# One state of each scan step in layer 3 multiplied with C by TensorE and ScalarE, and two small matmuls split over row groups

## The chip, the cores and the metric

The kernel runs on one core of a Trainium2 chip. The core has TensorE (PE, matmuls into PSUM), VectorE (DVE), ScalarE (ACT), GpSimd (POOL) and SyncE (SP, which here issues the DMA transfers). The engines run side by side, each through its own list of instructions in order, and wait for each other by semaphores. The metric is the device time of one execution in microseconds (us).

## The reference

Four layers are applied one after the other to an image of 8 x 64 x 64 x 64 float32. The change lies in layer 3, which holds two passes of a bidirectional selective scan: over one image axis, then over the other. For each direction, cut to what matters:

```
xn = rms_norm(x);  xz = xn @ ipw.T;  xc, z = split(xz)          # 64 -> 2 x 256 channels
xc = silu(causal_dwconv(xc))                                     # 4 taps along the sequence
dbl = xc @ xpw.T                                                 # 4 (dt) + 16 (B) + 16 (C) values per token
dt = softplus(dbl[:4] @ dtw.T + dtb)                             # 256 channels
h_t[d, n] = exp(dt_t[d] * A[d, n]) * h_{t-1}[d, n] + dt_t[d] * xc_t[d] * B_t[n]     # n = 0..15
y_t[d] = sum over n of h_t[d, n] * C_t[n]
y = (y + D * xc) * silu(z);  y @ opw.T
```

A sequence has 64 tokens. There are 256 inner channels d and 16 states n. C_t[n] depends on the token and the state only, not on the channel.

## The kernel before, in words

**Tiling.** Layer 3 works in *steps*: `steps` holds 2 passes (s) x 16 chunks (c) x 4 groups (g) x 2 directions (k) = 256 of them. A step takes 512 tokens (eight sequences) and all 256 channels of one direction. A tile is [128, 1024]: 128 channels on the partitions, and along the row 512 tokens of channels 0 to 127 (j = 0), then the same 512 tokens of channels 128 to 255 (j = 1). For each of the 16 states one such tile is worked through.

**The loop.** `stream` (line 433) is shared by layers 1, 2 and 3. Its iteration `i` is one state of one step, `i = 16 * step + n`; it writes out the order of all instructions by hand. Per state the work is:

- `fetch` (SP): the row of B and C of this state is loaded from HBM, broadcast to 128 partitions, six states ahead (tile `bc`, eight buffers).
- `multiply_b` (POOL, line 484): `hb = du * B`, three states ahead, four buffers.
- `decay` (ACT, line 491): `dA = exp(dt * A[n])`, two activations of 512, into one of two PSUM buffers, issued for state i + 2 at the end of iteration i.
- `scan` (DVE, line 500): the recurrence, over `dA` and `hb`. For most states its result overwrites `dA`. For a *shared* state it goes to an SBUF tile `h` (three buffers), so that the PSUM buffer is free as soon as the scan ends.
- `multiply_c` (line 514): the product with C. DVE does it for most states (into `hc`, four buffers) right after the scan; POOL does it for the states listed in `Step.shared`, in the next iteration, after that iteration's `multiply_b`.
- `gather` (PE, line 306): the product is added to the PSUM tile `acc` by two 128x512 matmuls with the identity, two iterations later. At state 0 of the next step it first drains the finished sum: `drain` (DVE, line 2074) multiplies `acc` with silu(z). At state 2 this stands behind the scan, and `acc` has one buffer.

In layer 3 the shared states are (1, 4, 7, 10, 13), and (2, 6, 10, 14) where k = 1 and g is odd.

**What else goes through the loop.** `prepare` (line 1999) computes the next step's inputs in pieces, one piece in an iteration, from state 1 on: tap matmuls (2009), silu to `u` (2021), the B, C, dt projection (2024), its copy `dbl` and its store to HBM (2027, 2030), the dt matmuls (2033, four rows of weights), softplus (415), `du` (POOL, 2044), the z matmuls (2047, 64 rows of weights), silu to `z` (2057). A piece of ACT work that needs another table of functions is marked `CALM` and is held back until `calm(i)` says that neither state i nor i + 1 is shared. Other pieces come from two queues that `advance` (line 417) steps once per iteration: `urgent`, in which `finish` (line 2087) stands once a k = 1 step is done (output matmuls 2093 and 2096, then an activation that writes the output tile, 2112), and `behind`, in which `begin` (line 1925) loads and normalises the next chunk. All these pieces share one PSUM tile `mm` (pool `pp`, one buffer of two banks): a piece that yields True holds it, and no other may take it until it is released.

Of the kernel before, what the change touches and what calls it, by code (L numbers as in the profile page):

```python
# [10 lines left out]
F32 = mybir.dt.float32  # L11
AF = mybir.ActivationFunctionType
ALU = mybir.AluOpType
# [5 lines left out]
C = 64  # L19
HW = 64  # L20
L = HW * HW
NS = 16
T = 1024
# [83 lines left out]
def layouts(i):  # L107
    o = {"x": i["x"].reshape(NP, 128, L)}
# [19 lines left out]
    p = "L1_conv_"  # L128
# [26 lines left out]
    p = "L2_conv_"  # L155
# [6 lines left out]
    xp = i[p + "ssm_xproj_w"]  # L162
# [12 lines left out]
    p = "L3_conv_"  # L175
# [8 lines left out]
    o["l3_xp"] = i[p + "x_proj_w"].reshape(4, 36, 2, 128).transpose(3, 0, 2, 1)  # L184
    o["l3_dtw"] = i[p + "dt_proj_w"].reshape(4, 256, 4).transpose(2, 0, 1)
# [83 lines left out]
class Net:  # L269
# [163 lines left out]
    def stream(self, pools, ahead, steps, behind, rest=None):  # L433
# [18 lines left out]
        nc = self.nc  # L452
        bp, hbp, hcp, hp, pe, pa = pools
        total = len(steps) * NS
        B, CC, hb, dA, hc, acc = {}, {}, {}, {}, {}, {}

        def need(i, what):

# [34 lines left out]
        def shared(i):  # L493
            return i % NS in steps[i // NS].shared

        def scan(i):
            s, n = steps[i // NS], i % NS
            h = hp.tile([128, T], F32, name="h") if shared(i) else dA[i]
            way = slice(None, None, -1) if s.rev else slice(None)
            nc.vector.tensor_tensor_scan(h[:, way], dA[i][:, way], hb.pop(i)[:, way], s.first(n), ALU.mult, ALU.add)  # L500
            dA[i] = h
            if shared(i):
                s.keep(n, h)

        def calm(i):

# [10 lines left out]

        def gather(i):
            at, n = divmod(i, NS)
            if n == 0:  # L520
                if at:
                    steps[at - 1].drain(acc.pop(at - 1))
                    steps[at - 1].done()
                acc[at] = pa.tile([128, T], F32, name="acc")
                begun[at] = steps[at].skip(acc[at])
            self.mm(acc[at], self.ident, hc.pop(i), start=n == 0 and not begun[at], stop=n == NS - 1)
# [12 lines left out]
        for i in range(total + 2):  # L539
            at, n = divmod(i, NS)  # L540
            need(i + ahead[0], "bc")
            need(i + ahead[1], "du")
            fetch_c(i + ahead[2])
            fetch(i + ahead[0])
            multiply_b(i + ahead[1])
            if 0 < i <= total and shared(i - 1):
                multiply_c(i - 1)


            first = i > NS and n == 2  # L550
# [12 lines left out]
            room = work is None or work.said is not True and (n < steps[0].early or hasattr(steps[at + 1], "du"))  # L563
            self.advance(behind, room, calm(i))
            if late:
                gather(i - 2)
            if i < total:
                scan(i)
            if first:
                gather(i - 2)  # L570
            if i < total:
                if not shared(i):
                    multiply_c(i)
            decay(i + 2)
        steps[-1].drain(acc.pop(len(steps) - 1))
# [288 lines left out]
    def layer1(self, src, dst):  # L864
        nc, tc, d = self.nc, self.tc, self.d
        mid = self.hbm["x1a"]
        with ExitStack() as ctx:
# [339 lines left out]

            class Step:
                start, early, late = 2, 8, True
                shared = (1, 4, 7, 10, 13)  # L1210
                shaped = staticmethod(lambda t: t)

                def __init__(self, b, k, j):
# [313 lines left out]
    def l2_scan(self, hx, hy):  # L1527
        nc, tc, d = self.nc, self.tc, self.d
        with ExitStack() as ctx:
# [35 lines left out]

            class Step:
                bc_shape, start, early, late = [128, 2, T], 2, 0, False
                shared = (1, 4, 7, 10, 13)
                rev = False
                behind = None  # L1570
                shaped = staticmethod(lambda t: t)
# [247 lines left out]
    def layer3(self, src, dst):  # L1819
# [8 lines left out]
        with ExitStack() as ctx:  # L1828
# [12 lines left out]
            class Weights:  # L1841
# [12 lines left out]
                def load(self):  # L1854
# [19 lines left out]
                    both = cp.tile([128, 2, 256], F32, name=f"both{s}")  # L1874
                    self.dtw, self.z = self.take("dtw", both[:4]), both[C:]
                    self.dtb, self.A, self.D = self.take("dtb"), self.take("A"), self.take("D")

                def build(self):
# [22 lines left out]
                                ALU.mult,  # L1901
                            )
                    for k in range(2):
                        nc.vector.tensor_scalar(
                            self.z[:, k, :], self.w_in[C:, k, 256:], self.nw[C:, k : k + 1], None, ALU.mult
                        )
# [74 lines left out]
            class Step:  # L1981
# [6 lines left out]
                def __init__(self, s, c, g, k):  # L1988
                    self.s, self.c, self.g, self.k, self.rev = s, c, g, k, k == 1
                    self.w = weights[s]  # L1990
                    self.shared = (2, 6, 10, 14) if k and g % 2 else (1, 4, 7, 10, 13)
                    self.lanes = [(slice(j * W, j * W + W), self.w.A[:, k, j, :]) for j in range(2)]

                def ready(self):
# [4 lines left out]
                def prepare(self):  # L1999
# [19 lines left out]
                    for j in range(2):  # L2019
                        at = slice(j * W, j * W + W)  # L2020
                        nc.scalar.activation(u[:, at], px[:, at], AF.Silu, bias=w.cb[:, k, j : j + 1])  # L2021
                    pd = pp.tile([128, T], F32, name="mm")[:36, :W]
                    for j in range(2):
                        nc.tensor.matmul(pd, w.xp[:, k, j, :], u[:, j * W : j * W + W], start=j == 0, stop=j == 1)  # L2024
                    yield True
                    dbl = p2.tile([36, W], F32, name="dbl")
                    nc.scalar.copy(dbl, pd)
                    self.bc = hp.tile([NS, 2, W], F32, name="bc")
                    for m in range(2):
                        nc.sync.dma_start(self.bc[:, m, :], dbl[4 + m * NS : 4 + m * NS + NS])  # L2030
                    pt = pp.tile([128, T], F32, name="mm")
                    for j in range(2):
                        nc.tensor.matmul(
                            pt[:, j * W : j * W + W], w.dtw[:, k, j * 128 : j * 128 + 128], dbl[0:4], start=True, stop=True
                        )
                    yield True
                    yield CALM
# [117 lines left out]
```

## Time and profile before

| | us |
|---|---|
| median of 3 runs | 24,518.06 (24,506.06 to 24,526.78) |
| the profiled execution | 24,525.61 |
| its span, first to last instruction | 24,523.8 |
| layer 3 within it | about 11,290 to 24,510 |

Busy shares of the whole span, from the page: PE 85%, DVE 91%, ACT 60%, POOL 90%. How to read it: engine rows give the line of the kernel, the operation, the tile written and the tiles read, the shapes and the count, then busy time and mean duration, then the idle time just before these instructions and what ended it. A float32 matmul appears as two `MATMUL` records (two passes), each with its weight load on the row of PEld. Matmul records are pipelined and overlap, so that the distance from start to start is what a pass costs. A timeline row gives the start, the duration, and in brackets how long the engine stood idle before it.

### The profile page before, as it was taken

The numbers are of one execution on the slowest core, as the hardware profiler recorded it, in microseconds if no ns is written. First come the engines' busy times: TensorE is split into PE (matmuls) and PEld (weight loads), VectorE is DVE, ScalarE is ACT, GpSimd is POOL, SyncE is SP. The second block draws the span as 40 slices with busy tenths as digits, with TensorE's granted clock in tenths as the row PEclk, the third lists the DMA queues.
The fourth block names the chain that finished last, engine by engine and source line by source line (L and its number), as shares of the span: only waits on it lengthen the run. The fifth ranks groups of instructions, "written<-read, shape, count | busy, mean of one in ns | idle before, by whom it ended". The sixth has DMA issues, their size and how long they took to land. (4 is left out here: it accounts for less than half of the span.)

```text
span 24523.8 us, 192937 instructions
## 1 busy us (share of the span) xinstructions
PE 20916.6 (85%) x53146; PEld 8080.3 (33%) x53146; DVE 22352.9 (91%) x12956; ACT 14733.5 (60%) x18824; POOL 22093.4 (90%) x10580
## 2 busy tenths in 40 slices
PE   7778888888888888898888888888888888888888
PEld 5323333333333223222333333333333333333333
DVE  5599999999999689978999999999999999999999
ACT  5445555555555456525666666666666666666666
POOL 0499999999999579967999999999999999999999
PEclk9889999999999999999999999999999999999999
DMA  2699889889888589923555555555555554555454
GB/s 76 198 328 319 314 314 322 313 314 318 315 311 310 173 284 338 321 54 120 173 168 171 171 172 168 172 170 170 171 169 172 170 172 169 172 169 173 168 174 157
DMA packets 1835292, 5282.68 MB, mean 215 GB/s; under 512 B 533712, under 2 KB 539924, under 8 KB 1831904
## 3 DMA queue, kind: packets, MB, share of 16 engines
q1 hardware_dynamic: 1809632, 5207.00, 62.8%
q10 hardware_dynamic: 24576, 63.33, 0.7%
q8 instruction: 423, 6.93, 0.1%
q14 instruction: 661, 5.41, 0.1%
HBM read 5112.85 MB, written 156.11 MB: 215 GB/s over the span
## 5 line engine op out<-in xcount | busy, mean ns | idle before, releaser
L484 POOL TENSOR_TENSOR hb<-du,bc 128x1024 f32<-128x1024 f32 x4608 | 10775.2, 2376 | 215.9 <-DVE h L500 143.7
L306 PE MATMUL acc<-hc,ident 128*128 128x512 f32 x18560 | 8782.1, 614 | 91.8 <-DVE img L1271 53.7
L491 ACT ACTIVATE dA<-dt,w_A 128x512 f32<-128x512 f32 x8192 | 5658.5, 691 | 3947.5 <-DVE hc L514 2892.5
L500 DVE TENSOR_TENSOR_SCAN dA<-dA,hb 128x1024 f32<-128x1024 f32 x3320 | 7579.2, 2283 | 199.0 <-ACT dA L491 114.9
L306 PE MATMUL acc<-h,ident 128*128 128x512 f32 x8064 | 4663.0, 707 | 2408.4 <-POOL h L514 2375.8
L306 PEld LDWEIGHTS acc<-hc,ident 128*128 128x128 f32 x18560 | 3638.5, 200 | 5214.5 <-issue 4560.6
L484 POOL TENSOR_TENSOR hb<-du,b 128x1024 f32<-128x1024 f32 x2048 | 4834.2, 2390 | 490.5 <-DVE dA L500 215.9
L514 DVE TENSOR_TENSOR hc<-dA,bc 128x1024 f32<-128x1024 f32 x3232 | 3954.9, 1224 | 244.7 <-issue 4.9
L491 ACT ACTIVATE dA<-dt,w_l_A 128x1024 f32<-128x1024 f32 x2560 | 2856.8, 1117 | 1001.4 <-DVE hc L514 761.1
L500 DVE TENSOR_TENSOR_SCAN h<-dA,hb 128x1024 f32<-128x1024 f32 x1416 | 3227.9, 2280 | 79.9 <-ACT dA L491 79.0
L514 POOL TENSOR_TENSOR h<-h,bc 128x1024 f32<-128x1024 f32 x1376 | 3264.8, 2373 | 8.0 <-DVE h L500 8.0
L306 PEld LDWEIGHTS acc<-h,ident 128*128 128x128 f32 x8064 | 1572.6, 213 | 5133.1 <-POOL h L514 3445.9
L500 DVE TENSOR_TENSOR_SCAN dA<-dA,carry,hb 128x1024 f32<-128x1024 f32 x1320 | 3093.1, 2343 | 116.5 <-POOL hb L484 45.1
L514 DVE TENSOR_TENSOR hc<-dA,c 128x1024 f32<-128x1024 f32 x1408 | 1722.9, 1224 | 116.8 <-DMA c<-bc 6.9
L514 POOL TENSOR_TENSOR h<-h,c 128x1024 f32<-128x1024 f32 x640 | 1518.5, 2373 | 8.2 <-ACT carry L1254 7.4
L491 ACT ACT_TABLE_LOAD x1128 | 1447.2, 1283 | 20.0
L500 DVE TENSOR_TENSOR_SCAN h<-dA,carry,hb 128x1024 f32<-128x1024 f32 x600 | 1404.2, 2340 | 36.6 <-ACT dA L491 25.5
L1254 ACT COPY carry<-dA 128x1 f32<-128x1 f32 x1056 | 167.6, 159 | 1646.7 <-DVE hc L514 1606.5
L2009 PE MATMUL mm<-xn,taps 128*128 128x512 f32 x2048 | 933.9, 598 | 1.1 <-ACT z L2057 1.1
L2044 POOL TENSOR_TENSOR du<-dt,u 128x1024 f32<-128x1024 f32 x256 | 607.6, 2374 | 9.8 <-ACT dt L415 9.8
L2024 PE MATMUL mm<-u,w_xp 128*36 128x512 f32 x1024 | 489.3, 600 | 139.1 <-ACT u L2021 132.3
L726 POOL MEMSET xf<- 128x24 f32 x33 | 4.3, 142 | 657.4 <-PE ps L747 494.4
(320 smaller groups left out, 17864.0 us busy)
## 6 DMA issues: line engine op xcount, KB each, us to landing
bc<-bc SPq DMA_DIRECT2D x4096, 512.0 KB
b<-bc SPq DMA_DIRECT2D x2048, 512.0 KB
c<-bc SPq DMA_DIRECT2D x2048, 512.0 KB
bc<-bc SPq DMA_DIRECT2D x512, 1024.0 KB
tmp<-rs SPq DMA_DIRECT2D x93, 512.0 KB
raw<-x SPq DMA_DIRECT2D x64, 512.0 KB
inv<-rs SPq DMA_DIRECT2D x64, 512.0 KB
tmp<-x SPq DMA_DIRECT2D x192, 128.0 KB
```

The lines of the kernel that those rows point to most:

```text
L306: self.nc.tensor.matmul(o, lhsT, r, start=start, stop=stop)
L484: nc.gpsimd.tensor_tensor(s.shaped(hb[i]), s.shaped(s.du), B.pop(i), ALU.mult)
L491: nc.scalar.activation(dA[i][:, cut], s.dt[:, cut], AF.Exp, scale=A[:, n : n + 1])
L500: nc.vector.tensor_tensor_scan(h[:, way], dA[i][:, way], hb.pop(i)[:, way], s.first(n), ALU.mult, ALU.add)
L514: engine.tensor_tensor(s.shaped(o), s.shaped(h), CC.pop(i), ALU.mult)
L726: nc.gpsimd.memset(x[:, :, HW:], 0.0)
L1254: nc.scalar.copy(self.carry[:, n : n + 1], h[:, last : last + 1])
L2009: nc.tensor.matmul(tokens(px[:, j * W : j * W + W]), w.taps[k][:, m, j * 128 : j * 128 + 128], xn[:, :, f : f + HW], start=m == 0, stop=m ...
L2024: nc.tensor.matmul(pd, w.xp[:, k, j, :], u[:, j * W : j * W + W], start=j == 0, stop=j == 1)
L2044: nc.gpsimd.tensor_tensor(du, dt, u, ALU.mult)
```

## The change

- Each step of layer 3 gets a list `turned = (13,)`. A turned state is scanned into an `h` tile like a shared one, but is multiplied with C in another way, by the generator `turn`: eight matmuls take 128x128 blocks of `h` as weights against the identity, so that the tile stands transposed in `mm`, tokens on the partitions; four activations on ACT copy it to SBUF, each scaled per partition by C of that token (`ct`); eight more matmuls with the copied blocks as weights turn it back and add it to `acc`.
- `turn` is put at the head of `urgent` when the state has been scanned. Its first piece takes the tile `mm` and yields `CALM`. Before the last state of the step is gathered, `gather` steps the queues until `turn` is over.
- The shared states become (1, 4, 7, 10), and (0, 3, 6, 9, 11) where k = 1 and g is odd. `calm` is unchanged.
- `ct` is loaded once per step from the stored C, 512 values of four bytes, as [128, 4].
- The dt matmuls use partitions 0 to 3 for the first 128 channels and 64 to 67 for the second (so the projection writes the four dt values twice, 68 rows); the z matmuls use partitions 0 to 63 and 64 to 127. The weights of both lie in one tile `both`.

Layers 1 and 2 have an empty `turned` list. In the changed kernel the lines are shifted: 2112 becomes 2153, 2074 becomes 2115, 306 becomes 307, 500 becomes 504.

```
@@ stream
+        def turned(i):
+            return i % NS in steps[i // NS].turned
+
         def scan(i):
             s, n = steps[i // NS], i % NS
-            h = hp.tile([128, T], F32, name="h") if shared(i) else dA[i]
+            h = hp.tile([128, T], F32, name="h") if shared(i) or turned(i) else dA[i]
...
+            if turned(i):
+                del CC[i]
+                turns[i] = Task(turn(i, dA.pop(i)))
+                self.urgent.appendleft(turns[i])
+
+        def turn(i, h):
+            s = steps[i // NS]
+            ps = s.pp.tile([128, T], F32, name="mm")
+            for m in range(4):
+                for j in range(2):
+                    at, o = j * 512 + m * 128, (m * 2 + j) * 128
+                    nc.tensor.matmul(ps[:, o : o + 128], h[:, at : at + 128], self.ident, start=True, stop=True)
+            yield CALM
+            o = hcp.tile([128, T], F32, name="hc")
+            for m in range(4):
+                at = slice(m * 256, m * 256 + 256)
+                nc.scalar.activation(o[:, at], ps[:, at], AF.Copy, scale=s.ct[:, m : m + 1])
+            yield False
+            for m in range(4):
+                for j in range(2):
+                    at, f = j * 512 + m * 128, (m * 2 + j) * 128
+                    nc.tensor.matmul(acc[i // NS][:, at : at + 128], o[:, f : f + 128], self.ident, start=False, stop=False)
...
         def gather(i):
             at, n = divmod(i, NS)
+            if turned(i):
+                return
+            if n == NS - 1:
+                for m in steps[at].turned:
+                    while not turns[at * NS + m].over:
+                        self.advance(behind)
...
-                if not shared(i):
+                if not shared(i) and not turned(i):
                     multiply_c(i)
@@ layer 3, Step
-                    self.shared = (2, 6, 10, 14) if k and g % 2 else (1, 4, 7, 10, 13)
+                    self.turned, self.pp = (13,), pp
+                    self.shared = (0, 3, 6, 9, 11) if k and g % 2 else (1, 4, 7, 10)
...
-                    pd = pp.tile([128, T], F32, name="mm")[:36, :W]
+                    pd = pp.tile([128, T], F32, name="mm")[:68, :W]
...
                     for j in range(2):
+                        at = slice(j * C, j * C + 4)
                         nc.tensor.matmul(
-                            pt[:, j * W : j * W + W], w.dtw[:, k, j * 128 : j * 128 + 128], dbl[0:4], start=True, stop=True
+                            pt[:, j * W : j * W + W], w.both[at, k, 128 - j * 128 : 256 - j * 128], dbl[at], start=True, stop=True
                         )
...
+                    self.ct = p2.tile([128, 4], F32, name="ct")
+                    for n in self.turned:
+                        nc.sync.dma_start(self.ct, self.bc[n, 1].rearrange("(m p) -> p m", p=128))
...
-                            w.z[:, k, j * 128 : j * 128 + 128],
-                            xn[C:, :, 4 : 4 + HW],
+                            w.both[j * C : j * C + C, k, j * 128 : j * 128 + 128],
+                            xn[j * C : j * C + C, :, 3 + j : 3 + j + HW],
```

More of the change, by code (lines that the diff above doesn't have):

```diff
@@ L183, in layouts @@
     o["l3_cb"] = i[p + "conv_b"].reshape(4, 2, 128).transpose(2, 0, 1)
-    o["l3_xp"] = i[p + "x_proj_w"].reshape(4, 36, 2, 128).transpose(3, 0, 2, 1)
-    o["l3_dtw"] = i[p + "dt_proj_w"].reshape(4, 256, 4).transpose(2, 0, 1)
+    xp = i[p + "x_proj_w"].reshape(4, 36, 2, 128).transpose(3, 0, 2, 1)
+    o["l3_xp"] = np.concatenate([fill(xp, (128, 4, 2, 64)), xp[..., :4]], axis=3)
+    o["l3_dtw"] = i[p + "dt_proj_w"].reshape(4, 2, 128, 4).transpose(3, 1, 0, 2)
     o["l3_dtb"] = i[p + "dt_proj_b"].reshape(4, 2, 128).transpose(2, 0, 1)
@@ L454, in stream @@
         total = len(steps) * NS
-        B, CC, hb, dA, hc, acc = {}, {}, {}, {}, {}, {}
+        B, CC, hb, dA, hc, acc, turns = {}, {}, {}, {}, {}, {}, {}
         def need(i, what):
@@ L1209, in layer1 @@
                 start, early, late = 2, 8, True
-                shared = (1, 4, 7, 10, 13)
+                shared, turned = (1, 4, 7, 10, 13), ()
                 shaped = staticmethod(lambda t: t)
@@ L1567, in l2_scan @@
                 bc_shape, start, early, late = [128, 2, T], 2, 0, False
-                shared = (1, 4, 7, 10, 13)
+                shared, turned = (1, 4, 7, 10, 13), ()
                 rev = False
@@ L1872, in load @@
                     self.cb, self.xp = self.take("cb"), self.take("xp")
-                    both = cp.tile([128, 2, 256], F32, name=f"both{s}")
-                    self.dtw, self.z = self.take("dtw", both[:4]), both[C:]
+                    both = self.both = cp.tile([128, 2, 256], F32, name=f"both{s}")
+                    for r in range(2):
+                        w = net.d["l3_dtw"][:, r, 2 * s : 2 * s + 2]
+                        nc.sync.dma_start(both[r * C : r * C + 4, :, 128 - r * 128 : 256 - r * 128], w)
                     self.dtb, self.A, self.D = self.take("dtb"), self.take("A"), self.take("D")
@@ L1903, in build @@
                     for k in range(2):
-                        nc.vector.tensor_scalar(
-                            self.z[:, k, :], self.w_in[C:, k, 256:], self.nw[C:, k : k + 1], None, ALU.mult
-                        )
+                        for r in range(2):
+                            at, o = slice(r * C, r * C + C), slice(r * 128, r * 128 + 128)
+                            nc.vector.tensor_scalar(
+                                self.both[at, k, o], self.w_in[at, k, 256 + r * 128 : 384 + r * 128], self.nw[at, k : k + 1], None, ALU.mult
+                            )
                     net.minus_exp(self.A)
@@ L2025, in prepare @@
                     yield True
-                    dbl = p2.tile([36, W], F32, name="dbl")
+                    dbl = p2.tile([68, W], F32, name="dbl")
                     nc.scalar.copy(dbl, pd)
```

## The prediction

> **What bounds the kernel now.** I read first the busy time of the stretch that the change touches. Layer 3 runs from 11,290 to 24,510 us; the columns are length, then busy time (and instructions) of PE, weight loads, DVE, ACT and POOL, clock, DMA share, GB/s.
>
> ```profile
> 11290.00:24510.00 13220.00, 11461.83 (x24020) 4361.02 (x24019) 12824.98 (x7262) 8947.03 (x11821) 13038.78 (x5691) 0.95 0.51 170
> ```
>
> POOL is busy 99%, DVE 97%. Which of the two sets the pace is seen in what each waits for: next come the groups of DVE and of POOL between 13,000 and 23,000 us, 193.6 steps of 51.65 us.
>
> ```profile
> L500 DVE TENSOR_TENSOR_SCAN dA<-dA,hb 128x1024 f32<-128x1024 f32 x2180 | 4975.4, 2282 | 10.2 <-ACT dA L491 6.7 <-POOL hb L484 3.0
> L514 DVE TENSOR_TENSOR hc<-dA,bc 128x1024 f32<-128x1024 f32 x2179 | 2666.6, 1224 | 166.3 <-issue 4.0 <-PE acc L306 0.9 <-PE mm L2024 0.4
> L500 DVE TENSOR_TENSOR_SCAN h<-dA,hb 128x1024 f32<-128x1024 f32 x921 | 2099.7, 2280 | 47.0 <-ACT dA L491 46.3 <-issue 0.4 <-POOL hb L484 0.3
> L2074 DVE TENSOR_TENSOR z<-acc,z 128x1024 f32<-128x1024 f32 x194 | 235.0, 1211 | 70.9 <-PE acc L306 70.2
> ```
>
> ```profile
> L484 POOL TENSOR_TENSOR hb<-du,bc 128x1024 f32<-128x1024 f32 x3100 | 7248.2, 2377 | 126.7 <-DVE h L500 98.4 <-DVE dA L500 28.1
> ```
>
> POOL waits 126.7 us for scans of DVE; DVE waits 3.3 us for POOL. So DVE sets the pace and POOL follows closely. DVE's true waits are 10.2 + 47.0 + 70.9 + 5.3 = 133 us, 176 us over the layer's 13,220 us; the rest of the 166.3 us is the 0.08 us between a scan and the product that reads it.
>
> The third view is the timeline around one output pass, a k = 0 step of the second half; start, duration, engine, line.
>
> ```profile
> 18042.61 2.27 DVE L500 TENSOR_TENSOR_SCAN dA<-dA,hb 128x1024 f32<-128x1024 f32 x1
> ...
> 18045.46 1.02 ACT L2057 ACTIVATE z<-mm 128x1024 f32<-128x1024 f32 x1
> ...
> 18047.55 3.65 PE L2096 MATMUL mm<-z,w_end 128*64 128x512 f32 x8
> 18047.90 1.42 ACT L491 ACTIVATE dA<-dt,w_A 128x512 f32<-128x512 f32 x2
> ...
> 18049.63 2.28 DVE L500 TENSOR_TENSOR_SCAN h<-dA,hb 128x1024 f32<-128x1024 f32 x1
> ...
> 18049.75 1.42 ACT L491 ACTIVATE dA<-dt,w_A 128x512 f32<-128x512 f32 x2 [0.43 <-DVE hc L514]
> ...
> 18051.83 2.27 DVE L500 TENSOR_TENSOR_SCAN dA<-dA,hb 128x1024 f32<-128x1024 f32 x1
> ...
> 18053.30 0.67 ACT L2112 ACTIVATE out<-mm,w_l_linb 64x512 f32<-64x512 f32 x1
> ```
>
> Scans start at states 11, 13 and 14. A state whose product with C is on DVE takes 3.50 us there; one that only scans takes 2.20 us (18049.63 to 18051.83). The decay of state i+2 (1.42 us on ACT) can start only when state i has left its PSUM buffer, and the scan starts 0.12 us after it ends: before a state that follows a scan-only state ACT has just 2.20 us, 0.66 us to spare.
>
> **The change on DVE and POOL.** State 13 leaves POOL in every step; for DVE it stays a scan-only state. In three of four steps DVE does what it did. In the fourth (k = 1, odd g) six states only scan instead of four, so two products go: 2 x (3.50 - 2.20) = 2.60 us, and the final product with z falls at a place 0.16 us cheaper: 2.76 x 64 steps = 177 us less. POOL loses one 2.32 us product in three steps and gains one in the fourth: 1.2 us per step on average, which shortens nothing by itself, as DVE hardly waits for it. But PE does: its long waits are for POOL's products, and they make PE late for the final product and for ACT's inputs.
>
> ```profile
> PE acc L306 <- POOL h L514: 1167.9, 537, 5.4
> ...
> DVE z L2074 <- PE acc L306: 70.2, 66, 2.5
> ```
>
> I take the 176 us as gone: the last POOL product ahead of a step's end is now 10 or 11, and POOL needs 21 x 2.32 = 48.7 us per ordinary step against DVE's 50.5. Ends: none of it, or all.
>
> **TensorE.** A 512-column matmul is two passes 0.43 us apart; state 13's two cost 1.72 us. Sixteen 128-column ones replace them. The nearest row is layer 0's, with a new 128x128 weight each time:
>
> ```profile
> 100.49 1.05 PE L634 MATMUL pt<-w_cent,x 128*128 128x128 f32 x8
> 101.38 1.03 PE L659 MATMUL py<-zt,w_ydft 128*128 128x512 f32 x2
> ```
>
> Eight passes in 0.89 us, 0.11 us each, so 32 cost 3.5 us. The other end is the load (0.19 us) added to each pass, 9.6 us. I take 0.11. The Trainium skill, "TensorE: Matmul & The Clock Gate", Part 3, The mechanism, says that a weight load overlaps running matmuls only where the row group differs. That speaks against this change, whose weights all use the full 128 rows; by it the turning would cost the 9.6 us. The row above shows full-row loads hidden, and the measurement decides.
>
> The dt and z matmuls gain, by the same form in layer 1:
>
> ```profile
> 4036.05 1.15 PE L1234 MATMUL mm<-dbl,w_l_dtw 4*128 4x512 f32 x4 [1.43 <-ACT dbl L1228]
> 4037.13 3.62 PE L306 MATMUL acc<-h,ident 128*128 128x512 f32 x4
> ```
>
> Four passes in 1.08 us against 1.72: 1.3 us per step for the two pairs. PE goes from 94 passes (40.6 us) to about 41.1 us of a 51.6 us step: no bound, and the gain is worth nothing by itself.
>
> **ScalarE: where it is paid.** The four 128x256 scalings: two 512-wide activations from PSUM take 1.27 us together, a 16-wide copy 0.21 us; so 0.45 us for one, 0.38 for each next, 1.6 us in all (ends 1.27, width alone, and 2.8, each as dear as a 512-wide one). In most steps they lie before the next step's decay 1, in a 2.1 us gap. What costs is elsewhere. `calm` asks only for `shared` states, and 13 is no longer one, so table loads and waits may now stand at states 12 and 13, though 13 is still scan-only.
>
> (a) Output pass. The built order has the activation of `finish` at state 12, ahead of the decay of 14, in every k = 0 step; it stood at state 14. Its matmuls cannot be earlier (they need the PSUM tile that z leaves at 18046.48) and end at 18051.20. ACT, free since 18049.32, waits; 0.67 us of output, 1.42 of decay, 0.14 of starts: scan 14 at 18053.47 instead of 18051.83, 1.64 us late. In the first half the strided output takes 1.13 us: 2.10 us. 64 x 1.64 + 64 x 2.10 = 239 us. Ends: 0 if the matmuls were ready, and 80 us more if the 2.5 us by which they come later in one of four such steps (18254.87 with z at 18251.34) stays.
>
> (b) z in the odd k = 1 step goes from state 11 to 12. From scan start to the end of the decay after the z block is 6.71 us above; with 0.12 scan 14 can start at 6.83, and is wanted at 3.50 + 2.20 = 5.70: 1.13 x 64 = 72 us. Ends: 0 and 72, all durations being from rows.
>
> (c) Before an odd k = 1 step, whose state 0 is shared, state 15 is not calm: scaling is forced at state 1 of that step. Counted from its first scan: decay 2 ends at 3.84, scaling at 5.45, the last turned pair at 5.93, state 15's sum at 7.65 (the z product wants it at 7.90: no wait), conv taps 11.09, skip 12.81, states 0 to 2 17.97, B/C projection 19.88, its copy on ACT 20.5, decay 7 21.9: scan 7 at 22.04 instead of 21.57, 0.47 x 64 = 30 us. Ends: 0, and 1.2 us more for scalings of 2.8.
>
> (d) At the end of those steps: shared 9 and 11 load POOL. Counting 2.32 us per product, state 11's ends at 45.1; PE adds 11, 12, turns 13; scaling from 50.6 to 52.2, the next step's decay 1 at 53.7, just as its scan at 53.8 wants it. For g = 3 two norm products (1.41 us each), flushed by `ready`, push it 1.9 us later: 32 x 1.9 = 61 us. Ends: 0 and 2.8 x 64 = 179.
>
> A RMS copy before decay 15 in g = 1, k = 0 adds 0.4 x 16 = 6 us. The load of C by token is 512 small pieces on SP's queue: 2048 pieces take 2.1 us there in the median, so 0.5 (1.4 at the longest); the B/C loads behind it run six states, 18 us, ahead. Nothing; without that lead it would be 0.5 us a step. It is issued three states after the stores it waits for.
>
> **Sum.** +239 + 72 + 30 + 61 + 6 - 177 - 176 = +55 us. The profiled execution took 24,525.6 us (span 23.8); 24,581, and that execution stands 7.5 us above the median: **24,573 us**.
>
> **Rivals.**
> 1. Output activation not late (faster): were the matmuls done by 18049.6, (a) vanishes: 24,334 us. For it: ACT has gaps. Against: 3.65 us of matmuls that start after z. It decides once most of 1.64 us is saved.
> 2. The old waits stay: PE keeps arriving late although POOL has fewer products. For it: DVE's 70 us for PE may have other causes. Up to 24,749 us; half of it, 24,661.
> 3. Turning not pipelined: 0.30 us a pass, scaling 3.0 us later in every odd k = 1 step (192 us), the turned-back pair 0.76 us later at the next (89 us in the z product and in (c)): 24,854 us. Against it: layer 0's row.
>
> **Chances.** Forecast 0.64 with its own range 24,480 to 24,650; rivals 0.12, 0.16, 0.08. About 0.2%, 49 us, is what a measurement can tell from no change, so slower begins at 24,567. Of the forecast's 0.64 I put 0.33 above, 0.29 within, 0.02 below. Slower 0.57, same 0.29, faster 0.14. The range leaves out rivals 1 and 3 and reaches from (c), (d) and some 40 us of (a) gone, 24,440, to rival 2, 24,750.
>
> **What would show it.** In the profile after: scan 14 waiting 1.6 to 2.1 us for a decay in k = 0 steps behind an output activation released by PE; 1.1 us at scan 14 of odd k = 1 steps; the z product hardly waiting; passes of the turn 0.11 us apart; DVE scans without a product on DVE 1344, not 1216, in layer 3. I am wrong if the output activation finds its matmuls ready, if z still waits, or if POOL shows up as DVE's releaser.

## The result, and the profile after

The changed kernel takes 24,803.53 us (median of 4 runs, 24,791.17 to 24,820.06) against 24,512.06 us (4 runs, 24,504.84 to 24,526.78) for the kernel before beside it: 1.0116 times the time, interval 1.0104 to 1.0129. The forecast was 24,573 us with a range up to 24,750: slower was right, but the loss is some 290 us instead of 55. The profiled execution took 24,820.06 us, its span 24,818.2; layer 3 (first scan to the end of the last product with z) grew from 13,222 to 13,522 us, by 300, so that the whole loss lies there.

Busy time of that layer in the changed kernel (length, then PE, weight loads, DVE, ACT, POOL with counts, granted clock with 1.00 for full speed, DMA share, GB/s):

```profile
11290.00:24800.00 13510.00, 11594.50 (x31145) 5032.18 (x31145) 12678.32 (x7132) 9324.89 (x12867) 12779.15 (x5561) 0.94 0.52 167
```

DVE does less work than before (12,678 us against 12,825) and takes longer over it. POOL is busy 95% instead of 99%. So neither engine's work grew: waits did. The groups of DVE and of POOL between 13,000 and 23,000 us name them:

```profile
L504 DVE TENSOR_TENSOR_SCAN dA<-dA,hb 128x1024 f32<-128x1024 f32 x2037 | 4651.2, 2283 | 350.7 <-ACT dA L492 279.3 <-POOL hb L485 65.9 <-issue 4.6
L504 DVE TENSOR_TENSOR_SCAN h<-dA,hb 128x1024 f32<-128x1024 f32 x994 | 2266.0, 2280 | 33.2 <-ACT dA L492 30.3 <-POOL xn L2008 1.7 <-POOL hb L485 0.8
L2115 DVE TENSOR_TENSOR z<-acc,z 128x1024 f32<-128x1024 f32 x189 | 228.9, 1211 | 78.4 <-PE acc L307 76.8
```

```profile
L485 POOL TENSOR_TENSOR hb<-du,bc 128x1024 f32<-128x1024 f32 x3030 | 7087.2, 2363 | 537.8 <-DVE h L504 332.7 <-DVE dA L504 199.7 <-DMA bc<-bc 2.4
```

The plain scans waited 10.2 us before and wait 350.7 now, for the decay on ACT; the product with z still waits for PE. POOL waits 538 us for DVE instead of 127, so POOL follows. (Where POOL is named as DVE's releaser, as at 23376.11 in the timeline below, it is the decay too: the scan starts right behind the first two of the ACT activations of L492, and POOL had finished that scan's product 7 us earlier.)

What ACT waits for is in the list of waits, same stretch (total, times, longest). Before, the output activation hardly waited:

```profile
ACT out L2112 <- PE mm L2096: 4.8, 12, 0.4
```

After:

```profile
ACT out L2153 <- PE mm L2137: 264.4, 93, 3.6
ACT hc L524 <- PE mm L519: 232.2, 93, 4.3
ACT sq L1984 <- PE mm L307: 104.1, 48, 3.0
```

All three are PE's. To sort the waits by place I took each DVE instruction's start, subtracted the usual distance from the one ahead of it (2.20 us behind a scan that is followed by a scan, 3.50 for scan and product) and summed what was over, by the state at which it stood, for all of layer 3:

| us of DVE waits in layer 3 | before | forecast | after |
|---|---|---|---|
| scan 14 of k = 0 steps (a) | 0 | 239 | 328.7 |
| scan 14 of odd k = 1 steps (b) | 0 | 72 | 68.9 |
| scan 7 of odd k = 1 steps (c) | 0 | 30 | 29.0 |
| state 1 (d) | 0 | 61 | 46.7, elsewhere |
| state 15 | 7.7 | 6 | 58.6 |
| product with z | 106.9 | 0 | 116.7 |
| states 6, 8, 10 and small ones | 70.9 | 0 | 25.7 |
| all | 185.5 | 408 | 674.3 |

674.3 - 185.5 is 489 us more of waits; 177 us of products that left DVE and 11 us of shorter gaps behind the reciprocal (0.52 to 0.16 us, 31 times) come off: 301, and the layer grew by 300. So the table accounts for the whole loss.

Now one output pass of the second half, from the timeline of the changed kernel:

```profile
23366.56 1.02 ACT L2098 ACTIVATE z<-mm 128x1024 f32<-128x1024 f32 x1
...
23367.64 1.08 PE L2134 MATMUL mm<-raw,w_res 64*64 64x512 f32 x2 [1.48 <-ACT z L2098]
...
23368.66 5.34 PE L2137 MATMUL mm<-z,w_end 128*64 128x512 f32 x8
...
23370.90 2.23 DVE L504 TENSOR_TENSOR_SCAN h<-dA,hb 128x1024 f32<-128x1024 f32 x1
...
23374.04 0.69 ACT L2153 ACTIVATE out<-mm,w_l_linb 64x512 f32<-64x512 f32 x1 [3.61 <-PE mm L2137]
...
23374.62 2.73 ACT L492 ACTIVATE dA<-dt,w_A 128x512 f32<-128x512 f32 x4
...
23376.11 2.30 DVE L504 TENSOR_TENSOR_SCAN dA<-dA,hb 128x1024 f32<-128x1024 f32 x1 [2.98 <-POOL hb L485]
```

The order is the forecast one: the output activation ahead of decay 14, waiting for its matmuls, scan 14 late. But the eight passes that took 3.65 us before take 5.34 here, and scan 14 is 2.98 us late instead of the 1.64 forecast for such a step. Why is in the columns of the granted clock, taken over three neighbouring stretches of 3.41 us:

```profile
23365.28:23368.69 3.41, 1.93 (x6) 0.28 (x4) 3.32 (x3) 3.38 (x4) 3.41 (x3) 1.00 0.79 282
23368.69:23372.10 3.41, 3.41 (x5) 0.93 (x5) 3.32 (x4) 1.69 (x3) 3.41 (x2) 0.50 0.11 41
23372.11:23375.52 3.41, 3.41 (x9) 1.28 (x8) 1.02 (x1) 1.45 (x3) 3.41 (x3) 1.00 0.94 326
```

In the first PE idled 1.48 us, waiting for ACT's z; in the second it ran at half clock; in the third it was back. By the starts of the passes, 73 of the layer's 128 output passes were slowed so (8 passes 4.75 us from first start to last instead of 3.06), and none of 128 before. Behind the 73 slow ones scan 14 was 3.3 us late in the mean, behind the others 1.6. Half clock altogether in layer 3, summed from the clock's record: 1,364 us before, 1,667 after.

The same thing makes the product with z wait, at the start of an odd k = 1 step, where the scaling is forced at state 1:

```profile
16730.54 1.95 PE L519 MATMUL mm<-ident,h 128*128 128x128 f32 x16
...
16732.33 1.88 PE L307 MATMUL acc<-hc,ident 128*128 128x512 f32 x4
...
16738.56 1.55 ACT L524 ACTIVATE hc<-mm,ct 128x256 f32<-128x256 f32 x4
...
16739.07 3.78 PE L529 MATMUL acc<-ident,hc 128*128 128x128 f32 x16 [4.86 <-ACT hc L524]
...
16742.64 2.28 PE L307 MATMUL acc<-hc,ident 128*128 128x512 f32 x4
...
16744.95 1.23 DVE L2115 TENSOR_TENSOR z<-acc,z 128x1024 f32<-128x1024 f32 x1 [2.07 <-PE acc L307]
```

PE turns the state in 1.95 us, has nothing to do for 4.86, and then turns it back at half clock in 3.78: the sum of state 15 comes behind it, and z waits 2.07 us. The clock there:

```profile
16739.00:16743.00 4.00, 3.93 (x17) 3.91 (x18) 3.79 (x3) 2.49 (x6) 4.00 (x3) 0.50 0.04 7
```

Of the 64 odd k = 1 steps, 44 had half clock within the 8 us ahead of the product with z. There z waited 1.85 to 3.1 us, 112.6 us in all; in the other 20 it waited 0.21 us at the most.

And with the normalising of a chunk: POOL's product keeps PE idle for 4.87 us, and the next passes run at half clock. They make the norm's matmuls late, which run at full speed again (1.87 us for four passes), and a copy on ACT ahead of decay 15 waits for them.

```profile
16563.91 3.78 PE L307 MATMUL acc<-h,ident 128*128 128x512 f32 x4 [4.87 <-POOL h L540]
...
16570.22 1.87 PE L307 MATMUL mm<-sq,mean 64*1 64x512 f32 x4
...
16572.14 1.00 ACT L1984 COPY sq<-mm 1x1024 f32<-1x1024 f32 x1 [2.68 <-PE mm L307]
...
16574.55 2.30 DVE L504 TENSOR_TENSOR_SCAN dA<-dA,hb 128x1024 f32<-128x1024 f32 x1 [1.39 <-ACT dA L492]
```

### The profile page after: what moved, and what is told of

Read it like the earlier page. It is cut to its first block, busy times and chain, and to the rows that moved or that the text cites. A ratio compares the mean times of both kernels' runs of the same rounds, so it can differ in the third digit from the quotient of the medians.

```text
span 24818.2 us, 208400 instructions
## 1 busy us (share of the span) xinstructions
PE 21067.9 (85%) x60314; PEld 8757.9 (35%) x60314; DVE 22213.3 (90%) x12832; ACT 15117.4 (61%) x19879; POOL 21838.8 (88%) x10452
## 5 line engine op out<-in xcount | busy, mean ns | idle before, releaser
L307 PE MATMUL acc<-hc,ident 128*128 128x512 f32 x18048 | 8586.2, 613 | 88.4 <-DVE img L1303 50.5
L504 DVE TENSOR_TENSOR_SCAN dA<-dA,hb 128x1024 f32<-128x1024 f32 x3192 | 7289.8, 2284 | 649.2 <-ACT dA L492 462.4
L492 ACT ACTIVATE dA<-dt,w_A 128x512 f32<-128x512 f32 x8192 | 5638.1, 691 | 3251.2 <-DVE hc L540 2284.8
L307 PE MATMUL acc<-h,ident 128*128 128x512 f32 x7552 | 4233.6, 689 | 1810.4 <-POOL h L540 1781.7
L307 PEld LDWEIGHTS acc<-hc,ident 128*128 128x128 f32 x18048 | 3486.9, 199 | 4793.1 <-issue 4193.9
L540 DVE TENSOR_TENSOR hc<-dA,bc 128x1024 f32<-128x1024 f32 x3104 | 3798.6, 1224 | 230.2 <-issue 5.8
L504 DVE TENSOR_TENSOR_SCAN h<-dA,hb 128x1024 f32<-128x1024 f32 x1544 | 3519.7, 2280 | 68.5 <-ACT dA L492 65.6
L492 ACT ACTIVATE dA<-dt,w_l_A 128x1024 f32<-128x1024 f32 x2560 | 2856.8, 1117 | 998.8 <-DVE hc L540 758.1
L540 POOL TENSOR_TENSOR h<-h,bc 128x1024 f32<-128x1024 f32 x1248 | 2943.7, 2359 | 2.5 <-DVE h L504 2.5
L504 DVE TENSOR_TENSOR_SCAN h<-dA,carry,hb 128x1024 f32<-128x1024 f32 x600 | 1404.6, 2341 | 37.7 <-ACT dA L492 27.6
L2061 PE MATMUL mm<-u,w_xp 128*68 128x512 f32 x1024 | 559.3, 674 | 276.6 <-ACT u L2058 276.6
L529 PE MATMUL acc<-ident,hc 128*128 128x128 f32 x4096 | 575.9, 300 | 251.2 <-ACT hc L524 251.2
L2111 PE MATMUL acc<-u,skip 128*128 128x512 f32 x1024 | 582.0, 697 | 233.3 <-DVE z L2115 232.8
```

What stands on the lines that cost most here:

```text
L307: self.nc.tensor.matmul(o, lhsT, r, start=start, stop=stop)
L492: nc.scalar.activation(dA[i][:, cut], s.dt[:, cut], AF.Exp, scale=A[:, n : n + 1])
L529: nc.tensor.matmul(acc[i // NS][:, at : at + 128], o[:, f : f + 128], self.ident, start=False, stop=False)
L540: engine.tensor_tensor(s.shaped(o), s.shaped(h), CC.pop(i), ALU.mult)
L2111: nc.tensor.matmul(acc[:, at], self.w.skip[self.k][:, j, :], self.u[:, at], start=True, stop=False)
```

## Experiments

Four explanations stood against each other. First, that of the forecast: it is the order on ACT, places (a) to (d), each with a fixed price. Second, PE's clock: PE has less to do, idles in longer pieces, and what follows a piece runs at half speed. Third, that the row groups alone cost something, by taking work off PE. Fourth, that with the waits gone POOL becomes the bound and caps any gain. Ratios below are to the kernel before on the same chip.

### The queues held off around the turned state (e1_calm)

```
-            return i + 1 >= total or not (shared(i) or shared(i + 1))
+            return i + 1 >= total or not (shared(i) or shared(i + 1) or turned(i) or turned(i + 1))
...
-                self.urgent.appendleft(turns[i])
+                self.urgent.insert(1 if self.held is self.urgent else 0, turns[i])
```

The output activation and z can no longer stand at states 12 and 13. The second line keeps a `finish` that still holds the tile `mm` ahead of the turn.

> The changed kernel, with states 12 and 13 closed to table loads and queue pieces, as state 13 was when it was shared: the output activation stands at state 14 again, z of the odd k = 1 step at state 14. In the changed kernel DVE waits 329 us before scan 14 of the k = 0 steps and 69 us before scan 14 of the odd k = 1 steps. Theory A (placement: the new time is in ACT pieces that stand ahead of decays a scan-only state needs, and in PE at half clock after long waits): these 398 us go, some 80 us come back because the scaling is forced to state 1 in one more of eight steps; 24,490 us (24,420 to 24,580). Theory B (the turning itself costs: its matmuls and scalings on PE and ACT): the waits move elsewhere, at least 24,700 us.

Measured: 24,622.07 us, 1.0039 (1.0026 to 1.0052). (a) is 0, (b) 14 us: the order on ACT was indeed the cause of both. But the time is 42 us above the range expected, and z waits 284.5 us for PE instead of 116.7. Two kinds of step make the difference. With `calm` stricter the scaling falls at state 1 behind 23 of the 32 k = 0 steps of g = 0 too, and z waits 82.9 us there. In the k = 1 steps of g = 1 the norm's four matmuls, which stood at state 14, now stand at state 2, between the turning back and state 15's sum; z waits 157.7 us there, 2.1 us a step at full clock and up to 7.3 us where half clock came on top. In the DVE groups between 13,000 and 23,000 us:

```profile
L504 DVE TENSOR_TENSOR_SCAN dA<-dA,hb 128x1024 f32<-128x1024 f32 x2065 | 4710.8, 2281 | 24.1 <-ACT dA L492 13.0 <-POOL hb L485 10.4
...
L2115 DVE TENSOR_TENSOR z<-acc,z 128x1024 f32<-128x1024 f32 x192 | 232.9, 1213 | 209.4 <-PE acc L307 209.4
```

Of 398 us that (a) and (b) cost, 384 went, and some 185 net were kept in the time: a wait removed at one end of the step came back in half at the other.

### The output matmuls shortened (e6_short)

```
-                nc.tensor.matmul(ps.rearrange("p (s t) -> p s t", t=HW), w.res, x, start=True, stop=False)
-                for k in range(2):
-                    for j in range(2):
-                        nc.tensor.matmul(
-                            ps, w.end[:, k, j, :], ys[k][:, j * W : j * W + W], start=False, stop=k == 1 and j == 1
-                        )
+                nc.tensor.matmul(ps.rearrange("p (s t) -> p s t", t=HW), w.res, x, start=True, stop=True)
```

The order stays; the eight passes of L2137 are left out.

> The changed kernel without the eight passes over the scan results in the output matmuls (the image gets its residual product alone, so the output lacks layer 3's scan). The order of everything else stays; the output activation still stands at state 12, but its matmuls end 3.4 us earlier. Theory A: DVE's wait before scan 14 of the k = 0 steps falls from 2.6 us on average to under 0.3 us, 24,490 us (24,450 to 24,540). Theory B: the wait is taken up by the next one, the time falls by less than 100 us, over 24,700 us.

Measured: 24,518.46 us, 0.9997 (0.9987 to 1.0006). (a) is 0 without a change of order: what scan 14 pays is the wait for these passes. z waits 9.8 us only. PE comes to the turning later here and stands idle at most 2.1 us ahead of turning back in the odd k = 1 steps (3.1 to 4.9 us in the changed kernel), and no z product had half clock in the 8 us ahead of it. There is a new 132 us before scan 15 of the k = 0 steps with a norm, where PE, now emptier still, does the norm's matmuls at half clock (ACT's copy L1984 waits 203 us between 13,000 and 23,000 us, against 104 after). Half clock in the layer is 1,756 us, the most of all runs, and yet the time is near that of the kernel before: what half clock costs depends on who waits behind it, not on its sum.

### More work for PE where it idled (e5_fill)

```
             yield CALM
+            if i + 3 < total and shared(i + 3):
+                for _ in range(2):
+                    for m in range(4):
+                        for j in range(2):
+                            at, f = j * 512 + m * 128, (m * 2 + j) * 128
+                            nc.tensor.matmul(ps[:, f : f + 128], h[:, at : at + 128], self.ident, start=True, stop=True)
...
                     pz = pp.tile([128, T], F32, name="mm")
-                    for j in range(2):
+                    for j in (0, 1) * (3 if k else 1):
                         nc.tensor.matmul(
                             tokens(pz[:, j * W : j * W + W]),
```

The z matmuls of the k = 1 step, which PE runs some us ahead of the output matmuls, are issued three times over, and so are the turning ones where the scaling is forced to state 1. Nothing useful is added.

> The changed kernel with more work on PE where it stands idle: the z matmuls of k = 1 steps are issued three times, and where the scaling is forced to state 1 the eight turning matmuls are issued three times (same values written again). Theory A with the clock (PE runs at half clock after a wait of some us, and that makes the output matmuls, the turned-back matmuls and the sum late): half-clock time in layer 3 falls from 1,662 us to under 1,450 us, DVE's wait for the sum before the z product from 117 us to under 40 us, the wait before scan 14 of k = 0 steps from 329 to about 240 us; 24,650 us (24,580 to 24,720). Theory B, or waits that have nothing to do with the clock: more PE work makes it equal or slower, 24,800 us or more.

Measured: 24,631.5 us, 1.0043 (1.0026 to 1.0059), against 1.0116 (1.0104 to 1.0129) without the idle work: the same useful work with more matmuls is 0.7% faster, some 180 us. In the layer (a) falls from 328.7 to 225.6 us, the z waits from 116.7 to 41.1, state 15 from 58.6 to 18.9, all waits from 674 to 477; half clock from 1,667 to 1,237. State 1 alone grew, from 46.7 to 76.2. The 41.1 us of z, just above the 40 expected, are not the clock's any more: 37.8 of them stand in the k = 1 steps of g = 1, where no z product had half clock in the 8 us ahead of it and the scaling waits up to 1.0 us for the added turning passes. An output pass of this kernel, from the timeline:

```profile
23201.66 1.09 PE L2140 MATMUL mm<-raw,w_res 64*64 64x512 f32 x2
...
23202.67 3.65 PE L2143 MATMUL mm<-z,w_end 128*64 128x512 f32 x8
...
23206.36 0.68 ACT L2159 ACTIVATE out<-mm,w_l_linb 64x512 f32<-64x512 f32 x1 [2.11 <-PE mm L2143]
```

3.65 us again, and ACT waits 2.11 instead of 3.61. None of the 128 output passes is slow, and PE's wait for ACT's z ahead of them, between 13,000 and 23,000 us, falls from 151.6 to 2.5 us. This is the clock shown as a cause and not only as company.

### The parts one by one (e3_rows, e4_turn)

The row groups alone, put into the kernel before:

```
-                            w.z[:, k, j * 128 : j * 128 + 128],
-                            xn[C:, :, 4 : 4 + HW],
+                            w.both[j * C : j * C + C, k, j * 128 : j * 128 + 128],
+                            xn[j * C : j * C + C, :, 3 + j : 3 + j + HW],
```

The dt matmuls get the same, with the 68 rows of the projection.

> The kernel before with the dt and z matmuls in two row groups and nothing else of the change. PE loses some 1.3 us of work per step. Theory A: worth nothing, within 25 us of the kernel before. Theory C (the row groups are to blame, since PE with less work falls to half clock more often): at least 50 us slower than before, half-clock time in layer 3 up from 1,359 us by 100 us or more.

Measured: 24,502.52 us, 0.9991 (0.9982 to 1.0000). Alone they cost nothing, and a gain is not clear of noise; the clock does fall (half clock 1,515 us against 1,364, and 27 of 128 output passes are slow), but there the output activation stands at state 14 and has time (2.0 us of waits in 10,000).

The changed kernel without the row groups, that is with the diff above undone:

> The changed kernel with the dt and z matmuls as before, in one row group. Theory A with the clock: PE has 1.3 us more work per step and falls to half clock less (under 1,600 us in layer 3 instead of 1,667), so the output matmuls and the scaling are late by less: 24,740 us (24,680 to 24,800). Theory C' (the row groups' saved PE time shortens what waits for PE): slower than the changed kernel by 30 us or more.

Measured: 24,688.98 us, 1.0059 (1.0046 to 1.0073). So beside the turn the row groups cost 0.57%, some 140 us, though alone they cost none. Two rows of its list of waits between 13,000 and 23,000 us, which stand at 232.2 and 264.4 us in the changed kernel:

```profile
ACT hc L523 <- PE mm L518: 204.3, 95, 4.5
ACT out L2147 <- PE mm L2131: 185.0, 96, 2.0
```

The output activation waits at most 2.0 us instead of 3.6, and none of the 128 passes is slow; (a) is 207.5 us, and half clock in the layer 1,086 us instead of 1,667. The gap ahead of the output matmuls is shorter: between 13,000 and 23,000 us PE waits there for ACT's z 52.8 us, at most 1.0, against 151.6, at most 2.2, in the changed kernel. That fits z matmuls which are longer without the row groups (1.98 us for four passes in the kernel before, 1.14 in the changed one) and push what PE does next towards the output pass; in e5_fill, where the z matmuls of these steps are issued three times, the gap was closed. The z waits stay (118.5 us): they do not come from the row groups.

### Only where products leave DVE (e9_odd)

```
-                    self.turned, self.pp = (13,), pp
-                    self.shared = (0, 3, 6, 9, 11) if k and g % 2 else (1, 4, 7, 10)
+                    self.turned, self.pp = (13,) if k and g % 2 else (), pp
+                    self.shared = (0, 3, 6, 9, 11) if k and g % 2 else (1, 4, 7, 10, 13)
```

The turn pays on DVE in one step of four; in the other three it only takes a product from POOL. Here it is left to the one.

> The changed kernel with state 13 turned in the odd k = 1 steps alone, where DVE loses two products; the other three of four steps keep state 13 on POOL, as before. No output activation stands at state 12. Theory A with DVE alone as the bound: 24,512 - 177 + 69 (z at state 12) + some 80 for late scaling, 24,430 to 24,500 us. Theory D, POOL takes over: 88 products and 2.8 us of norm products per four steps at 2.32 us are 51.75 us a step, as long as a step took before: 24,520 to 24,600 us, with DVE waiting for POOL's hb.

Measured: 24,534.6 us, 0.9998 (0.9989 to 1.0007). (a) is 0, but POOL has its old work and one product more in one step of four:

```profile
L485 POOL TENSOR_TENSOR hb<-du,bc 128x1024 f32<-128x1024 f32 x3101 | 7247.8, 2375 | 15.4 <-DVE h L504 14.9
```

15.4 us of waits in 10,000: POOL is full, and the scans wait for it (32.4 us in that stretch, against 3.0 before). The 177 us saved on DVE come back as waits. (b) stands at 69.1. State 1 stands at 82.4, of which 79.4 fall at the place of (d), 2.56 at the start of 31 chunks. z waits 124.1, 17 more than before. But POOL, busy 9,985 of the 10,000 us, would leave no room for the gain without these waits either. So the fourth explanation holds for this kernel: POOL's relief in the other three steps was costed at nothing by itself, and without it POOL is the bound.

### The places put right (e7_best, e8_bestfill, e10_norows)

e7_best has the two lines of e1_calm, and

```
-                    self.shared = (0, 3, 6, 9, 11) if k and g % 2 else (1, 4, 7, 10)
+                    self.shared = (1, 3, 6, 9, 11) if k and g % 2 else (1, 4, 7, 10)
...
                 if last:
-                    yield False
                     nc.sync.dma_start(dst[q, rows] if s == 0 else dst[q, rows, part * 4 * W : (part + 1) * 4 * W], images[b])
```

With no step sharing its state 0, the scaling stands ahead of state 1 everywhere, at state 15 or 0 by the trace. The last edit issues the store of the image one iteration earlier. No run separates these two edits.

> The changed kernel with states 12 and 13 closed to table loads and queue pieces, the odd k = 1 steps' shared states at (1, 3, 6, 9, 11) instead of (0, 3, 6, 9, 11), so that state 15 is open for the scaling in every step, and the output's store issued without waiting one iteration, so that the turning starts one iteration earlier at the end of a chunk. Theory A: the 398 us before scan 14 go and the scaling at state 15 leaves the z product nearly nothing to wait for (117 us in the changed kernel, 285 us where the scaling was forced to state 1 more often); some 200 us of waits stay, as many as the kernel before has, and the 177 us of products taken from DVE show: 24,360 us (24,290 to 24,450). Theory B (the turning costs as much as it saves): 24,500 us or more.

Measured: 24,433.34 us, 0.9954 (0.9942 to 0.9967): faster than both kernels, by 104 us than before (between the medians) and by 1.6% than the change. Scans into `h` and the z product in its DVE groups, same stretch:

```profile
L504 DVE TENSOR_TENSOR_SCAN h<-dA,hb 128x1024 f32<-128x1024 f32 x1025 | 2337.5, 2280 | 150.0 <-ACT dA L492 148.6 <-POOL hb L485 0.6
L2115 DVE TENSOR_TENSOR z<-acc,z 128x1024 f32<-128x1024 f32 x196 | 236.5, 1206 | 0.0
```

z never waits, and POOL is not the bound: its products with B wait 252.6 us in this stretch, nearly all for scans. 268.9 us of waits are left in the layer, 179.4 of them at state 1: the scaling, ahead of decay 1 on ACT, waits for PE's turn (485.6 us of such waits between 13,000 and 23,000 us, of which most pass in ACT's free time). The wait forecast under (d), after the chunk's last step, is among them: 79.5 us, 2.56 in each of 31.

e8_bestfill is e7_best with the z matmuls of k = 1 three times, e10_norows is e7_best without the row groups.

> The version before this one with the z matmuls of the k = 1 steps issued three times, 2.2 us more PE work in half of the steps. Theory A: half-clock time falls, but nothing on DVE's path waits for the output matmuls any more, so within 30 us of the version without. Theory C (the clock itself costs, wherever it falls): 50 us or more faster.

> The mended version (states 12 and 13 closed, shared states (1, 3, 6, 9, 11) in the odd k = 1 steps, store at once) without the row groups: dt and z matmuls as in the kernel before. PE has 1.3 us more work per step. Theory A with the clock: half-clock time in layer 3 falls from 1,182 to under 1,000 us; of DVE's 269 us of waits those for a late scaling at state 1 (some 90 us beside the 80 us at the end of a chunk, which are POOL's) may shrink; 24,430 us on the chip of the last runs less 0 to 60 us, a ratio to the kernel before of 0.993 to 0.996. Theory C' (with nothing late any more, less PE work is a gain again): ratio 0.997 or more.

Measured: 24,424.71 us, 0.9953 (0.9939 to 0.9967), and 24,424.7 us, 0.9956 (0.9943 to 0.9970). Neither differs from e7_best beyond noise, though half clock falls from 1,182 to 1,057 and 905 us. The sum of DVE's waits stays as it is (267.8 us in e10_norows against 268.9): what is left did not move with PE's clock, and the row groups bring nothing that shows.

## Why the prediction was wrong, step by step

- **Direction.** Slower was right, and for the reasons given first: the output activation in front of decay 14, z in front of it in odd k = 1 steps, `calm` not counting the turned state. e1_calm removed the rule, and (a) and (b) with it.
- **Floor of DVE.** 177 us less: the balance of the layer closes to 1 us with it. Scans without a product on DVE: 1,344, as said.
- **(a), forecast 239, measured 328.7: the step that failed.** I took the output matmuls at the 3.65 us of the kernel before. 73 of 128 of them ran at half clock. Where they ran at full clock, with the same order, (a) was 207.5 (e4_turn) and 225.6 us (e5_fill). So the mechanism was right and the sum within 15% at full clock, and the duration was not a constant. (The terms written for one step add up to 18,053.43, not 18,053.47; over all steps that is 5 us.)
- **(b) and (c) at scan 7.** Forecast 72 and 30, measured 68.9 and 29.0.
- **(c) at the product with z, forecast "no wait", measured 116.7 us.** A wait of z was named as a sign of being wrong, and it came. The same fault: I counted the turned-back passes at 0.11 us each and the sum of state 15 at 1.72 us. After its idle 4.86 us PE needed 3.78 us for the sixteen and 2.28 for the sum. I had counted how long PE would work but not how long it would stand before it.
- **(d), forecast 61, measured 46.7 in other steps.** In the place I named there is no wait in the changed kernel, so that the two amounts are near by chance. In its stead the scaling waits for PE after the even k = 1 steps:

```profile
16673.24 3.78 PE L307 MATMUL acc<-h,ident 128*128 128x512 f32 x4 [4.88 <-POOL h L540]
...
16683.11 1.57 ACT L524 ACTIVATE hc<-mm,ct 128x256 f32<-128x256 f32 x4 [4.26 <-PE mm L519]
...
16686.09 2.29 DVE L504 TENSOR_TENSOR_SCAN h<-dA,hb 128x1024 f32<-128x1024 f32 x1 [1.65 <-ACT dA L492]
```

  Again PE idle for 4.88 us, four passes in 3.78, the turn late. The wait I named is absent in the changed kernel and in e4_turn, 27.3 us in e5_fill, 55.0 in e1_calm, and 79.4 and 79.5 in e9_odd and e7_best. Why is open: in the changed kernel those steps reach the place later by the other waits, which gives POOL time, but no run varied that alone.
- **State 15, forecast 6, measured 58.6.** The copy L1984 of steps that I had not counted, the k = 1 steps of g = 1 (48.5 us): its norm matmuls come late behind passes at half clock; with the idle work of e5_fill state 15 stands at 18.9.
- **The old waits, 176 taken as gone.** Those at states 6 and 10 (60.1 us) and three of the four kinds of place of the z product (57.1 of 106.9) are gone. At the fourth, the start of the last kind of step, 49.8 us became 89.1; the extra turning passes of e5_fill bring it to 3.3, so what stands there now is the clock. The start of the k = 1 steps of g = 1, 0.4 us before, is new with 27.6 us. This is rival 2 in its sign only, by another cause.
- **Price of a turned pass.** 0.11 us was right at full clock: sixteen passes from 16730.54 to 16732.33, each with a new full-row weight. At half clock it was 0.22 (16739.07 to 16742.64). So rival 3 fell, and with it, for these shapes, what the Trainium skill says in "TensorE: Matmul & The Clock Gate", Part 3, The mechanism, that a load overlaps running matmuls only where the row group differs. (The same section also names a background weight buffer as a case in which a load is pulled ahead; these rows do not show which case they are.) Four scalings took 1.55 us against the 1.6 counted.
- **"The gain is worth nothing by itself", of the row groups.** True alone (e3_rows) and once the order is right (e10_norows). False in this kernel: without them the gap ahead of the output matmuls was shorter and no output pass slow (e4_turn), and they cost some 140 us.

In the layer's sum the forecast's +55 becomes: +90 in (a), +117 at z, -14 at state 1, +53 at state 15, -4 in (b) and (c), +26 at other states, -10 for old waits that were larger than taken, -11 behind the reciprocal: +302, measured 300. Of the 247 us between the two, (a), z and state 15 make 260, the rest nearly cancels; at these three places the timelines show matmuls at half clock ahead of the wait. e5_fill took some 180 us back with idle work alone, in the time, and 197 in the waits. In the changed kernel the part of the z waits at the start of the k = 1 steps of g = 1 is the clock as well: 23.5 of its 27.6 us stand in the 12 steps that had half clock, and the other 20 waited 0.21 us each.

## What to carry to other kernels

A matmul's duration in a trace holds for the idle time ahead of it there: when a change takes work off TensorE or puts a wait in front of it, look up the granted clock behind the nearest row with such a gap, and cost what follows at half speed wherever another engine waits for it. Where a queue's rule says when work may stand between others (here `calm`), ask whether the rule still names the right places when a new kind of state joins; but forbidding places moves work, so price the place where it lands before counting the gain. An engine's relief that is worth nothing today, POOL's here, may be what keeps it from being the bound after the next mend.

## What was unexpected of the hardware

- The clock halves after less idleness than I would have thought. In the changed kernel's layer 3 there are 374 stretches at half clock; the longest idle piece of PE in the 3.41 us ahead of each was 1.4 us at the least and 2.6 in the median. The record knows only 1.0 and 0.5; 260 of the 374 last 3.413 us, 112 twice that. The Trainium skill ("TensorE: Matmul & The Clock Gate", Why this matters for your kernels) advises no idle gaps above some 3 us; here 1.48 us in one 3.41 us stretch was followed by a half-clock one. The 1.4 us is the least that was seen and no threshold: other stretches at full speed held up to 2.0 us of idleness and were followed by full speed.
- Useless matmuls made the kernel faster: 1.0043 against 1.0116 of the time before.
- The price of one edit depended wholly on its company: the row groups changed the time by nothing clear of noise alone (0.9991), by +0.57% beside the turn, and again by nothing clear of noise once the order was mended.
